# Two layers on one core: the counts of a search on TensorE, another layout of B, and the loads and stores at both ends

## The chip, the core and the metric

The kernel is one program on one core of a Trainium2 chip. Its metric is the time of one execution on the device, in microseconds (us). Engines are called as in the profile: PE (TensorE), PEld (its weight loads), DVE (VectorE), ACT (ScalarE), POOL (GpSimd), SP (SyncE, which here issues the DMAs that are not by index).

## The reference

The input is 8 sequences of 256 tokens with 128 channels, 2048 tokens in all, in float32. Two layers follow each other. Each normalizes its tokens (mean and variance over the channels), gives the result to an attention-like part and to a mixture of experts, and adds both to its input:

```
xn = layernorm(x)
x  = x + attn0(xn) + ffn0(xn)
xn = layernorm(x)
x  = x + attn1(xn) + ffn1(xn)
```

`attn0` is a state-space scan: a second layer norm, an up-projection to 256 channels, a causal convolution over 4 tokens and a silu give `xm`. From `xm` one product gives `delta` (softplus, 256 channels) and B and C (16 numbers each for every token). For each channel and each of 16 states a first-order recurrence runs over the 256 tokens of a sequence:

```
h = exp(delta*A) * h + xm * (exp(delta*A) - 1) / (delta*A) * delta * B
y = sum over the 16 states of C * h
```

`y` times a gate goes through a down-projection. `ffn0` has 8 experts, and each expert chooses its 512 best tokens by softmax score; its output, times the score, is added to those rows. `attn1` is a retention with 8 heads, a decay mask, a norm by head and a gate. `ffn1` has 16 experts, and each token goes to its two best.

## The kernel before

**Start (L184–L330).** The 2048 tokens lie as 16 columns of 128 partitions (`x`, tile of 128x16x128; token = column*128 + partition). Four DMAs load x (L187), then SP goes on with A_log and the weights (L124). DVE takes statistics of each column (L233, L234), with the two operations on A between columns 7 and 8 (L231, L232); normalized copies are transposed on PE. The router's scores `sc` (128x8x16, experts by columns) are ready at the end of this stage (L740 and the lines after it).

**The search (`search`, L428–L455).** The 512 best tokens of each of 8 experts are found by looking for the threshold score bit by bit, 3 bits a step, in ten steps. A step has 7 candidates for each expert. DVE forms them (`cand`, L431), compares all scores with all candidates (`ge`, 128 x 7x8x16, bf16, L435) and sums over the 16 columns (`cp`, L441). The generator yields here; when it is called again, PE sums over the partitions with one product with a matrix of ones (`pc`, L444), and DVE keeps the candidates with at least 512 tokens (`keep`, L449), counts them (`m`, L452) and sets three bits of the threshold (L453). `cand` and the threshold live in unused columns of the PSUM tile `py`, which PE's sums over the states also write. In the profile they appear as `py`.

**Fronts (`front(q)`).** The tokens are worked in four blocks q of 512 (two sequences each). A front computes what the scan needs of one block: `pu` (L314, up-projection and convolution in one), `pg` (L327, the gate), `pd` (L353, for delta), and `pbc` (B and C, copied to `BC`, 32x512, L368). `C` goes to DRAM (`C_d`, L369), whence SP loads it again spread over all partitions (`Cb`, L644). `BT` holds B by tokens: partition r of 128, 8 chunks of 64 tokens, 18 numbers each. Rows 0 to 63 hold the 64 tokens of a chunk with their 16 values at columns 2 to 17, rows 64 to 127 hold the same 64 tokens with their values at columns 0 to 15; a window of two columns then gives each half of the partitions its own two of four states. The front fills it with 16 products of 16x64 with the identity (`pbt`, L383, 8 chunks for each half of the partitions), and two copies on ACT (L388). After that come the transposes of `xm` (`pxT`, L393), the copy `xT` on ACT (L401) and two DMAs (L402, L403) that write `xS`, which is `xT` with its halves of the partitions swapped. On ACT the logarithm of softplus (`w`, L375) stands ahead of the copies of BT; on DVE its operand `z` (L374) stands ahead of it. POOL and DVE finish `delta` (L406, L408).

**Units of the scan.** A unit is one sequence b, four states g and 128 channels dc: 64 units, and 8 for each sequence. `spread_b` (POOL, L657) puts columns of BT on diagonals (`Bd`), PE multiplies them by xT and xS (`u`, L673), ACT computes the decays (`ab`, L684, four exponentials), DVE computes `u` (L692) and runs the recurrence (`h`, L696), POOL multiplies it by `Cb` (L700), and PE adds the states up (`py`, L709). `down` (L726) follows for each sequence.

**Order.** In this layer the order on PE, ACT, DVE and POOL is that of the program, written out by hand; each engine takes its instructions in that order, and SP its DMAs too. Front 0 runs before the loop, and at every second of its yields, up to the tenth, the search does a step. Then the loop runs over the units k. It issues unit k's `u` and `h`, the products of k+1, the sums of k−2, C of k−1, the decays and `Cb` of k+2 and `Bd` of k+4, and then one part of each generator that runs: the search until it is done, the front of the next block (from k = 0, 16 and 32), the selection of an expert's rows (`select`, one begun every 5 units), whose tokens POOL gathers (`xg`, L548), and the experts' products, whose results POOL adds to rows of `acc_d` (L572).

PSUM tiles named by `bank(...)` take turns in two buffers: pu, pg, pd, pbt, pxT and pc are among them.

**Second layer (L866 and on).** Retention, then 47 tiles of 128 rows through the 16 experts. The rows come back by index into `y_d` (L1221), two for each token. POOL also scatters the rows to their tiles (L1150).

**End (L1305–L1315).** `x1` is a tile of 128x16x128, laid out as `x` was. For each of four quarters SP loads the two outputs for its tokens (`y`, L1311, 256 KB each), after all scatters; DVE adds them (L1314); SP stores the quarter (L1315).

Of the kernel before, what the change touches and what calls it, by code (L numbers as in the profile page):

```python
# [10 lines left out]
BF16 = mybir.dt.bfloat16  # L11
AF = mybir.ActivationFunctionType
ALU = mybir.AluOpType
AX = mybir.AxisListType
PSUM = bass.MemoryType.PSUM

P = 128
NB = 8
L = 256
NT = NB * L  # L20
NC = NT // P
DM = 128
D = 256
ND = D // P
N = 16
K = 4
E0 = 8
# [16 lines left out]
BK = 64  # L44
# [6 lines left out]
def block_kernel(ctx: ExitStack, tc: tile.TileContext, a: dict, out: bass.AP):  # L51
    nc = tc.nc

    def bc(ap, axis, n):
# [16 lines left out]
    ident = const.tile([P, P], F32, name="ident")  # L71
# [6 lines left out]
        out=triu, in_=ones, compare_op=ALU.is_gt, fill=0.0, base=0,  # L78
# [7 lines left out]
    ones_b = const.tile([P, P], BF16, name="ones_b")  # L86
# [52 lines left out]
    def after_all(i, *groups):  # L139

        for g in groups:
            for j in g:
                tc.add_manual_dep(
                    i.ins, j.ins.name,
                    mybir.DependencyInfo(mybir.DependencyClass.Sync, mybir.DependencyReason.DATA),
                    reason="rows by index",
                )


    with ExitStack() as l0:  # L150
        ET = mybir.EngineType
        l0.enter_context(tc.manual_schedule(engines={ET.PE, ET.Activation, ET.DVE, ET.Pool}))
        main = l0.enter_context(tc.tile_pool(name="main", bufs=1))
# [8 lines left out]
        def bank(name, shape):  # L162
            return ps_m.tile(shape, F32, name=name, tag="m")
# [18 lines left out]
            return load(*args, pool=main)  # L182

        x = main.tile([P, NC, DM], F32, name="x", tag="c8")  # L184
        xv = a["x"].rearrange("(c p) d -> p c d", p=P)
        for q in range(4):
            nc.sync.dma_start(x[:, 4 * q : 4 * q + 4, :], xv[:, 4 * q : 4 * q + 4, :])  # L187
        alog = load0("alog", [P, ND, N], a["alog"].rearrange("(c p) n -> p c n", p=P))
# [10 lines left out]
        NK = (1 << SB) - 1  # L199
# [74 lines left out]
        for h in range(2):  # L274
            for g in range(2):
                q = 2 * h + g
# [26 lines left out]
        def front(q):  # L303
            cols = slice(q * BLK, (q + 1) * BLK)
            win = slice(2 * q, 2 * q + 2)
            xq = main.tile([P, ND, BLK], F32, name=f"xm{q}", tag="xm")
# [69 lines left out]
            BTq = main.tile([P, 8, N + 2], F32, name=f"BT{q}", tag="BT", bufs=2)  # L376
            BT[q] = BTq

            pbt = bank(f"pbt{q}", [P, 8, N + 2])
            own = [(slice(0, BK), slice(2, N + 2)), (slice(BK, P), slice(0, N))]  # L380
            for rows, at in own:
                for j in range(8):
                    nc.tensor.matmul(  # L383
                        pbt[rows, j, at], BC[0:N, j * BK : (j + 1) * BK], ident[0:N, 0:N],
                        start=True, stop=True,
                    )
            for rows, at in own:
                nc.scalar.copy(BTq[rows, :, at], pbt[rows, :, at])  # L388
            for i in range(2):
                px = bank(f"pxT{q}_{i}", [P, 2, D])  # L390
                for c in range(2):
# [37 lines left out]
        def search():  # L429
            for i in range(30 // SB):  # L430
                nc.vector.tensor_tensor(  # L431
                    cand, bc(thr, 1, NK), bc(bits[:, i, :], 2, E0), ALU.bitwise_or
                )
                ge = main.tile([P, NK, E0, NC], BF16, name=f"ge{i}", tag="ge")
                nc.vector.tensor_tensor(  # L435
                    ge, bc(sc, 1, NK), bc(cand.bitcast(F32), 3, NC), ALU.is_ge
                )

                cp = main.tile([P, NK, E0], BF16, name=f"cp{i}", tag="cp", bufs=2)
                with nc.allow_low_precision(reason="whole numbers up to 16"):  # L440
                    nc.vector.tensor_reduce(cp, ge, AX.X, ALU.add)  # L441
                yield
                pc = bank(f"pc{i}", [P, NK, E0])
                nc.tensor.matmul(  # L444
                    pc.rearrange("p k e -> p (k e)"), ones_b, cp.rearrange("p k e -> p (k e)"),
                    start=True, stop=True,
                )
                keep = main.tile([P, NK, E0], I32, name=f"keep{i}", tag="keep", bufs=2)
                nc.vector.tensor_scalar(keep, pc, CAP - 0.5, None, ALU.is_ge)  # L449
                m = main.tile([P, E0], I32, name=f"m{i}", tag="m", bufs=2)  # L450
                with nc.allow_low_precision(reason="whole numbers up to 7"):
                    nc.vector.tensor_reduce(m, keep.rearrange("p k e -> p e k"), AX.X, ALU.add)  # L452
                nc.vector.scalar_tensor_tensor(  # L453
                    thr, m, 30 - SB * (i + 1), thr, ALU.logical_shift_left, ALU.bitwise_or
                )  # L455
# [847 lines left out]


    yv = y_d[0 : 2 * NT, :].rearrange("(k p c) d -> p k c d", p=P, k=2)  # L1305
    ov = out.rearrange("(c p) d -> p c d", p=P)
    for q in range(4):
        y = work.tile([P, WB], F32, name=f"y{q}", tag="wb", bufs=AHEAD)
        y = y[:, 0 : 8 * DM].rearrange("p (k c d) -> p k c d", k=2, c=4)
        for k in range(2):  # L1310
            after_all(nc.sync.dma_start(y[:, k], yv[:, k, quarter[q], :]), put)  # L1311
        xq = x1[:, quarter[q], :]
        for k in range(2):
            nc.vector.tensor_add(xq, xq, y[:, k])  # L1314
        nc.sync.dma_start(ov[:, quarter[q], :], xq)  # L1315


# [70 lines left out]
def _layout(i):  # L1388
    import numpy as np

    c = lambda v: np.ascontiguousarray(np.asarray(v))
    t = lambda v: np.ascontiguousarray(np.asarray(v).T)
    wll, bll = np.asarray(i["L0_attn_W_ll"]), np.asarray(i["L0_attn_b_ll"])
    return {
        "x": c(i["L0_attn_X"]).reshape(NT, DM),
        "ln_g": c(i["L0_attn_ln_g"]).reshape(DM, 1),
        "ln_b": c(i["L0_attn_ln_b"]).reshape(DM, 1),
        "wup1": t(i["L0_attn_W_up1"]),
        "wup2": t(i["L0_attn_W_up2"]),
        "conv_w": t(c(i["L0_attn_conv_w"]).reshape(D, K)),  # L1400
        "bits": np.array(
            [[(k + 1) << (30 - SB * (j + 1)) for k in range((1 << SB) - 1)] for j in range(30 // SB)],
            np.int32,
        ),
        "conv_b": _columns(i["L0_attn_conv_b"]),
        "wll": t(wll),
        "bll_d": _columns(bll[:D]),
        "bll_bc": c(bll[D:]).reshape(2 * N, 1),
        "b2x": _blocks(i["L0_ffn_b2"]),
        "alog": c(i["L0_attn_A_log"]),  # L1410
        "wdown": t(i["L0_attn_W_down"]),
        "bdown": c(i["L0_attn_b_down"]),
        "wr0": c(i["L0_ffn_Wr"]),
        "w1_0": c(i["L0_ffn_W1"]),
        "b1_0": _columns(i["L0_ffn_b1"]),
        "w2_0": c(i["L0_ffn_W2"]),
        "wq0": _heads(i["L1_attn_Wq"], 0),
        "wq1": _heads(i["L1_attn_Wq"], 1),
        "wk0": _heads(i["L1_attn_Wk"], 0),
        "wk1": _heads(i["L1_attn_Wk"], 1),  # L1420
        "wvT": t(_heads(i["L1_attn_Wv"], None)),
        "cen": np.eye(P, dtype=np.float32) - _mean(),
        "avg": _mean(),
        "w1a": c(i["L1_attn_W1"]),
        "w2a": c(i["L1_attn_W2"]),
        "gn_w": c(i["L1_attn_gn_w"]).reshape(DM, 1),
        "gn_b": c(i["L1_attn_gn_b"]).reshape(DM, 1),
        "decay": _decay(),
        "wr1": c(i["L1_ffn_Wr"]),
        "br1": c(i["L1_ffn_br"]),  # L1430
        "bank": _banks(i["L1_ffn_W1"], i["L1_ffn_b1"], i["L1_ffn_W2"]),
        "b2_1": c(i["L1_ffn_b2"]),
    }
# [18 lines left out]
```

## Time and profile before

| what | value |
|---|---|
| time before, median of 6 runs | 687.72 us |
| lowest and highest of them | 683.97 and 691.09 us |
| time of the profiled execution | 686.88 us |
| span of the profiled execution | 685.2 us |
| mean granted clock of PE | 0.869 |
| cp (L441) | 10 of 1.09 us on DVE |
| pc (L444) | 10 products of 0.19 us |
| pbt (L383), block 0 | 32 PE rows, 3.19 us |
| copies of BT (L388) | 2 a block, 0.52 us together (block 3) |
| the last addition (L1314) begins | 681.20 us |

The profile is of one execution, taken by the hardware profiler. Its span is what the engines' records cover, and the time beside it is that execution's own; the median is over other executions. A row of a timeline gives start, duration, engine, line, operation, output and inputs, shapes and the count; brackets give the idle time of the engine before it and what ended that. Matmuls are pipelined, and a product in float32 shows as two matmuls. The granted clock is TensorE's, as a share of full speed. "q" behind an engine's name means its queue of DMA issues. The lines of the profile are shown in the prediction.

### The profile page before, as it was taken

The numbers are of one execution on the slowest core, as the hardware profiler recorded it, in microseconds if no ns is written. First come the engines' busy times: TensorE is split into PE (matmuls) and PEld (weight loads), VectorE is DVE, ScalarE is ACT, GpSimd is POOL, SyncE is SP. The second block draws the span as 40 slices with busy tenths as digits, with TensorE's granted clock in tenths as the row PEclk, the third lists the DMA queues.
The fourth block names the chain that finished last, engine by engine and source line by source line (L and its number), as shares of the span: only waits on it lengthen the run. The fifth ranks groups of instructions, "written<-read, shape, count | busy, mean of one in ns | idle before, by whom it ended". The sixth has DMA issues, their size and how long they took to land.

```text
span 685.2 us, 14527 instructions
## 1 busy us (share of the span) xinstructions
PE 546.0 (80%) x5721; PEld 415.7 (61%) x5721; DVE 432.0 (63%) x669; ACT 332.2 (48%) x763; POOL 383.8 (56%) x320
## 2 busy tenths in 40 slices
PE   0897768779989889979887975496449989999980
PEld 0666555667755667755766764353125579999880
DVE  7377898997855777756868695664026543554343
ACT  2646346447487756687763750262003234555430
POOL 5004555686988789977899895107730023344240
PEclk9996798889999899999999997577558899999995
DMA  7914001222396242332332220124215237888305
GB/s 210 109 24 124 32 32 55 91 93 82 84 199 138 82 101 71 94 93 69 91 97 50 72 68 6 62 93 157 95 59 155 94 112 261 269 302 299 112 28 188
DMA packets 59859, 76.27 MB, mean 111 GB/s; under 512 B 14992, under 2 KB 43808, under 8 KB 59536
## 3 DMA queue, kind: packets, MB, share of 16 engines
q1 hardware_dynamic: 51632, 65.81, 33.2%
q0 software_dynamic: 8160, 9.54, 6.5%
q8 instruction: 45, 0.74, 0.4%
q14 instruction: 22, 0.18, 0.1%
HBM read 59.46 MB, written 13.78 MB: 107 GB/s over the span
## 4 chain that ended last, share of the span: by engine, by line
PE 50%; DVE 20%; ACT 8%; issue 8%; another core or an unknown queue 6%; POOL 3%; DMA 3%; SPq 1%; DVEq 0%; POOLq 0%; ACTq 0%
PE ph L1201 6%; PE py L709 5%; PE py L1215 5%; PE u L673 5%; DVE h L696 5%; PE ph L606 4%; DVE u L692 4%; PE pu L314 4%; PE po L624 2%; ACT ab L684 2%; PE pd L353 2%; POOL h L700 2%; PE ps L1034 2%; DVE st L1041 2%
## 5 line engine op out<-in xcount | busy, mean ns | idle before, releaser
L700 POOL TENSOR_TENSOR h<-h,Cb 128x1024 f32<-128x1024 f32 x64 | 169.5, 2744 | 35.2 <-DVE h L696 19.9
L696 DVE TENSOR_TENSOR_SCAN h<-ab,u 128x1024 f32<-128x1024 f32 x64 | 146.3, 2287 | 5.9
L684 ACT ACTIVATE ab<-delta,An 128x256 f32<-128x256 f32 x256 | 108.5, 497 | 19.3 <-DVE h L696 18.5
L1221 POOL DMA_INDIRECT y_d<-yo,xt x47 | 45.5, 968 | 118.6 <-DVE yo L1220 105.4
L692 DVE SCALAR_TENSOR_TENSOR u<-ab,u 128x1024 f32<-128x1024 f32 x64 | 77.8, 1216 | 37.9 <-ACT ab L684 14.8
L709 PE MATMUL py<-h,dg 64*64 64x128 f32 x2048 | 78.9, 295 | 18.3 <-POOL h L700 12.5
L673 PE MATMUL u<-Bd,xT 64*128 64x128 f32 x512 | 81.1, 304 | 14.4 <-DVE h L696 14.0
L673 PEld LDWEIGHTS u<-Bd,xT 64*128 64x128 f32 x512 | 68.6, 206 | 25.2 <-issue 9.7
L709 PEld LDWEIGHTS py<-h,dg 64*64 64x64 f32 x2048 | 62.4, 145 | 33.1 <-POOL h L700 17.0
L673 PE MATMUL u<-Bd,xS 64*128 64x128 f32 x512 | 79.3, 305 | 1.8 <-DMA xS<-xT 1.8
L1206 ACT ACTIVATE hid<-ph,wb 128x128 f32<-128x128 f32 x188 | 53.5, 368 | 48.7 <-issue 20.4
L673 PEld LDWEIGHTS u<-Bd,xS 64*128 64x128 f32 x512 | 66.6, 206 | 2.1 <-DMA xS<-xT 2.1
L1041 DVE TENSOR_TENSOR st<-ps,decay_sb 128x384 f32<-128x384 f32 x64 | 31.1, 547 | 55.6 <-remote 32.3
L572 POOL DMA_INDIRECT acc_d<-oc,idx x32 | 51.5, 1609 | 16.9 <-ACT oc L629 8.6
L1150 POOL DMA_INDIRECT xs_d<-xk,pos x32 | 32.0, 1001 | 41.9 <-DVE hit L1132 32.5
L1201 PE MATMUL ph<-xT,wb 128*128 128x128 f32 x376 | 52.9, 286 | 2.9 <-DVE xT L1195 2.7
L657 POOL TENSOR_TENSOR Bd<-eye,BT 128x256 f32<-128x256 f32 x64 | 52.4, 1051 | 0.0
L1201 PEld LDWEIGHTS ph<-xT,wb 128*128 128x128 f32 x376 | 48.0, 200 | 5.9 <-DVE xT L1195 3.1
L1215 PE MATMUL py<-wb,hid 128*128 128x128 f32 x376 | 49.5, 275 | 0.0
L624 PE MATMUL po<-w,ht 128*128 128x128 f32 x256 | 39.5, 296 | 10.8 <-ACT z L358 2.6
L624 PEld LDWEIGHTS po<-w,ht 128*128 128x128 f32 x256 | 33.8, 199 | 22.1 <-ACT ht L611 8.1
L1215 PEld LDWEIGHTS py<-wb,hid 128*128 128x128 f32 x376 | 45.7, 192 | 0.0
(257 smaller groups left out, 896.8 us busy)
## 6 DMA issues: line engine op xcount, KB each, us to landing
wb<-in_bank_dram SPq DMA_DIRECT2D x47, 514.0 KB
Cb<-C_d SPq DMA_DIRECT2D x32, 512.0 KB
w<-in_w_dram SPq DMA_DIRECT2D x16, 256.0 KB
xs_d<-zrow SPq DMA_DIRECT2D x1, 3031.5 KB
xt<-xs_d SPq DMA_DIRECT2D x11, 260.0 KB
xS<-xT SPq DMA_DIRECT2D x16, 128.0 KB
y<-y_d SPq DMA_DIRECT2D x8, 256.0 KB
decay_sb<-in_decay_dram SPq DMA_DIRECT2D x1, 1536.0 KB
```

Of the source, the lines that this page charges most:

```text
L572: i = nc.gpsimd.indirect_dma_start(out=acc_d, out_offset=bass.IndirectOffsetOnAxis(ap=idx[:, e, s : s + 1], axis=0), in_=oc, in_offset=Non ...
L624: nc.tensor.matmul(po, ht[:, hc, s * P : (s + 1) * P], w2[:, hc, :], start=(hc == 0), stop=(hc == NH - 1),)
L657: nc.gpsimd.tensor_tensor(t[:, w], eye.unsqueeze(1).unsqueeze(1).to_broadcast([P, 2, 2, BK]), bc(BT[b // 2][:, j + 2 * i : j + 2 * i + 2, ...
L673: nc.tensor.matmul(U[k][:, 2 * r : 2 * r + 2, t0 : t0 + BK], xT[b][r ^ half][rows, c, dc * P : (dc + 1) * P], Bd[b, g][rows, 2 * c + half] ...
L684: nc.scalar.activation(ab[k][:, n, :], delta[b // 2][:, dc, (b % 2) * L : (b % 2 + 1) * L], AF.Exp, scale=An[:, dc, g * NG + n : g * NG + ...
L692: nc.vector.scalar_tensor_tensor(U[k], ab[k], -1.0, U[k], ALU.add, ALU.mult)
L696: return nc.vector.tensor_tensor_scan(hf, af, uf, 0.0, ALU.mult, ALU.add)
L700: nc.gpsimd.tensor_mul(hh[k][:, w], hh[k][:, w], Cb[b, g][:, w])
L709: nc.tensor.matmul(pyv[cols, i, dc, :], dg[rows, dc, g * NG + n, :], hh[k][rows, n, j * P : (j + 1) * P], start=(g == 0 and dc == 0 and n ...
L1201: nc.tensor.matmul(ph[:, hc, :], w[:, hc * P : (hc + 1) * P], xTs[t], start=True, stop=True)
L1206: nc.scalar.activation(hids[t][:, hc, :], ph[:, hc, :], AF.Relu, bias=w[:, DI + NH * DM + hc : DI + NH * DM + hc + 1],)
L1215: nc.tensor.matmul(py, hids[t][:, hc, :], w[:, DI + hc * DM : DI + (hc + 1) * DM], start=(hc == 0), stop=(hc == NH - 1),)
```

## The change

1. The search no longer sums over the columns on DVE (`cp` and L441 go). PE forms `pc` with 16 products that add up in PSUM, one for each column of `ge`; the moving operand of each has 56 numbers in steps of 16 (32 bytes apart). They stand where the one product stood.
2. `pbt` is made by four products of 128 tokens, all partitions at once, in place of 16 of 64. A chunk with an even number then lies in rows 0 to 63, one with an odd number in rows 64 to 127. ACT copies each to its own half of BT, and two DMAs on SP (64 partitions, 4 pieces of 64 bytes each) copy each half's chunks to the other half.
3. At the end, the eight loads of y are issued ahead of the four stores, and the four quarters of y are held at once.
4. The input and the output are handed over by partition: a partition's share of x (16 tokens of 128) is contiguous in DRAM, and so is a partition's share of the output. The reordering lies outside of the kernel's time.

```diff
--- before.py
+++ after.py
@@ -182,7 +182,7 @@
             return load(*args, pool=main)
 
         x = main.tile([P, NC, DM], F32, name="x", tag="c8")
-        xv = a["x"].rearrange("(c p) d -> p c d", p=P)
+        xv = a["x"]
         for q in range(4):
             nc.sync.dma_start(x[:, 4 * q : 4 * q + 4, :], xv[:, 4 * q : 4 * q + 4, :])
         alog = load0("alog", [P, ND, N], a["alog"].rearrange("(c p) n -> p c n", p=P))
@@ -376,16 +376,17 @@
             BTq = main.tile([P, 8, N + 2], F32, name=f"BT{q}", tag="BT", bufs=2)
             BT[q] = BTq
 
-            pbt = bank(f"pbt{q}", [P, 8, N + 2])
-            own = [(slice(0, BK), slice(2, N + 2)), (slice(BK, P), slice(0, N))]
-            for rows, at in own:
-                for j in range(8):
-                    nc.tensor.matmul(
-                        pbt[rows, j, at], BC[0:N, j * BK : (j + 1) * BK], ident[0:N, 0:N],
-                        start=True, stop=True,
-                    )
-            for rows, at in own:
-                nc.scalar.copy(BTq[rows, :, at], pbt[rows, :, at])
+            pbt = bank(f"pbt{q}", [P, 4, N])
+            for c in range(4):
+                nc.tensor.matmul(
+                    pbt[:, c, :], BC[0:N, c * P : (c + 1) * P], ident[0:N, 0:N],
+                    start=True, stop=True,
+                )
+            up, low = slice(0, BK), slice(BK, P)
+            nc.scalar.copy(BTq[up, 0:8:2, 2:], pbt[up])
+            nc.scalar.copy(BTq[low, 1:8:2, 0:N], pbt[low])
+            nc.sync.dma_start(BTq[up, 1:8:2, 2:], BTq[low, 1:8:2, 0:N])
+            nc.sync.dma_start(BTq[low, 0:8:2, 0:N], BTq[up, 0:8:2, 2:])
             for i in range(2):
                 px = bank(f"pxT{q}_{i}", [P, 2, D])
                 for c in range(2):
@@ -435,16 +436,14 @@
                 nc.vector.tensor_tensor(
                     ge, bc(sc, 1, NK), bc(cand.bitcast(F32), 3, NC), ALU.is_ge
                 )
-
-                cp = main.tile([P, NK, E0], BF16, name=f"cp{i}", tag="cp", bufs=2)
-                with nc.allow_low_precision(reason="whole numbers up to 16"):
-                    nc.vector.tensor_reduce(cp, ge, AX.X, ALU.add)
                 yield
                 pc = bank(f"pc{i}", [P, NK, E0])
-                nc.tensor.matmul(
-                    pc.rearrange("p k e -> p (k e)"), ones_b, cp.rearrange("p k e -> p (k e)"),
-                    start=True, stop=True,
-                )
+                for c in range(NC):
+                    nc.tensor.matmul(
+                        pc.rearrange("p k e -> p (k e)"), ones_b,
+                        ge.rearrange("p k e c -> p (k e) c")[:, :, c],
+                        start=(c == 0), stop=(c == NC - 1),
+                    )
                 keep = main.tile([P, NK, E0], I32, name=f"keep{i}", tag="keep", bufs=2)
                 nc.vector.tensor_scalar(keep, pc, CAP - 0.5, None, ALU.is_ge)
                 m = main.tile([P, E0], I32, name=f"m{i}", tag="m", bufs=2)
@@ -1303,15 +1302,18 @@
 
 
     yv = y_d[0 : 2 * NT, :].rearrange("(k p c) d -> p k c d", p=P, k=2)
-    ov = out.rearrange("(c p) d -> p c d", p=P)
+    ov = out.rearrange("(p c) d -> p c d", p=P)
+    ys = []
     for q in range(4):
         y = work.tile([P, WB], F32, name=f"y{q}", tag="wb", bufs=AHEAD)
         y = y[:, 0 : 8 * DM].rearrange("p (k c d) -> p k c d", k=2, c=4)
         for k in range(2):
             after_all(nc.sync.dma_start(y[:, k], yv[:, k, quarter[q], :]), put)
+        ys.append(y)
+    for q in range(4):
         xq = x1[:, quarter[q], :]
         for k in range(2):
-            nc.vector.tensor_add(xq, xq, y[:, k])
+            nc.vector.tensor_add(xq, xq, ys[q][:, k])
         nc.sync.dma_start(ov[:, quarter[q], :], xq)
 
 
@@ -1392,7 +1394,7 @@
     t = lambda v: np.ascontiguousarray(np.asarray(v).T)
     wll, bll = np.asarray(i["L0_attn_W_ll"]), np.asarray(i["L0_attn_b_ll"])
     return {
-        "x": c(i["L0_attn_X"]).reshape(NT, DM),
+        "x": c(c(i["L0_attn_X"]).reshape(NC, P, DM).transpose(1, 0, 2)),
         "ln_g": c(i["L0_attn_ln_g"]).reshape(DM, 1),
         "ln_b": c(i["L0_attn_ln_b"]).reshape(DM, 1),
         "wup1": t(i["L0_attn_W_up1"]),
@@ -1448,4 +1450,5 @@
     with tile.TileContext(nc) as tc:
         block_kernel(tc, args, out)
     r = _run(nc, [arrays], core_ids=[0])
-    return r.results[0]["out_0_dram"].reshape(NB, L, DM)
+    y = r.results[0]["out_0_dram"].reshape(P, NC, DM)
+    return y.transpose(1, 0, 2).reshape(NB, L, DM)
```

## The prediction

> **What bounds the kernel now.** Three views, in this order: the page's busy shares and chain of waits; the timeline of the scan loop's first units, where the search runs; the timelines around B's copies and at the end.
>
> ```profile
> PE 546.0 (80%) x5721; PEld 415.7 (61%) x5721; DVE 432.0 (63%) x669; ACT 332.2 (48%) x763; POOL 383.8 (56%) x320
> PE 50%; DVE 20%; ACT 8%; issue 8%; another core or an unknown queue 6%; POOL 3%; DMA 3%; SPq 1%; DVEq 0%; POOLq 0%; ACTq 0%
> ```
>
> TensorE carries half of the chain, VectorE a fifth. Work moved from VectorE to TensorE gains only where VectorE ends last. All three parts touch short stretches, so I read each stretch by itself. The search runs at 35–101 us; this is one unit of the scan loop with one step in it:
>
> ```profile
> 85.08 1.09 DVE L435 TENSOR_TENSOR ge<-sc,py 128x896 bf16<-128x896 f32 x1
> 86.20 1.09 DVE L441 TENSOR_REDUCE cp<-ge 128x56 bf16<-128x896 bf16 x1
> 86.31 1.10 PE L709 MATMUL py<-h,dg 64*64 64x128 f32 x32 [1.19 <-POOL h L700]
> 87.20 1.22 DVE L692 SCALAR_TENSOR_TENSOR u<-ab,u 128x1024 f32<-128x1024 f32 x1
> 87.35 1.99 PE L314 MATMUL pu<-XnT,wcv 128*128 128x256 f32 x8
> 88.59 2.29 DVE L696 TENSOR_TENSOR_SCAN h<-ab,u 128x1024 f32<-128x1024 f32 x1
> 89.18 0.19 PE L444 MATMUL pc<-cp,ones_b 128*128 128x56 bf16 x1
> 90.80 0.19 DVE L449 TENSOR_SCALAR keep<-pc 128x56 int32<-128x56 f32 x1
> ```
>
> (Columns: start, duration, engine, line, output and inputs, count, and in brackets the idle time before and what ended it.) The count waits on PE behind py and pu, and ends at 89.37, 1.43 us before the scan lets DVE reach keep. So DVE sets this unit, with 1.09 us of cp in its row.
>
> **The change part by part.**
>
> *Count products.* Each of ten steps loses cp (1.09 us on DVE) and its one product becomes 16 accumulating ones: 15 more weight loads and matmuls a step, 150 of each in all, at the same place in PE's order. A bf16 product read in steps of 32 bytes is nowhere in this trace. The nearest row is
>
> ```profile
> 131.59 0.57 PE L535 MATMUL pi<-rr,ol 128*32 128x32 bf16 x16
> ```
>
> 16 bf16 products with 32 weight and 32 moving columns, spaced (0.57−0.176)/15 = 0.026 us. With 128+56 columns in place of 32+32 that is 0.026×184/64 = 0.076 us, my value: 15×0.076 = 1.13 us a step at full clock, 2.27 at half. The low end is the row itself (0.026, 0.4 us a step); the high end is the router's L740, whose fp32 products cost 6.83/32 = 0.213 us (3.2 us a step). I take the scaled row, since its type and form are nearest.
>
> [...]
>
> Before the loop (front of block 0, 35.7–63.6 us) PE is the path: pu, pc, pu, pc, pg, pd follow without gaps but for keep (0.32 and 0.34 us), as pg and pd wait for the PSUM bank that keep releases. The first count has 0.96 us of slack before the next pu (+0.2); the next two shift everything by 1.1 each: +2.2 up to BC at 55.03. From there DVE gains cp back: z no longer stands behind cp at 56.68, so the logarithm behind it on ACT comes 2.2−1.09 = 1.1 later, and so do the copies of BT. Taken on below.
>
> In the loop five steps remain (counts at 70.08, 73.58, 83.84, 89.18, 97.55). DVE's row a unit with a step goes from 6.9 to 5.8. PE's row is not free to run ahead: py writes the PSUM tile that holds the candidates, so it waits for ge. From keep: 2.1 us to the end of ge, py 1.05 (2.0 at half clock), pu 2.0 (2.85), pc 0.2: 5.35, or 7.15 at half clock. With 15 more products: 6.5 or 9.4. So before the larger is 6.9 (7.15), after 6.5 (9.4): −0.45 at full clock, +2.2 at half; one unit without pu in it −1.1; the first unit, still on PE's path at half clock, +1.0. The granted clock was 0.50 at 57–68, 0.85 at 74–77, 0.50 at 77–80, 0.63 at 80–84, 1.00 at 84–93, 0.66 at 93–98 us. Over the five I get **+0.2** (−4.4 with 0.026 us everywhere, +5 at 0.12). It breaks even where 15 spacings eat the 6.9−5.35 = 1.55 us: 0.10 us a product.
>
> *B.* 16 products of 64x16 become four of 128x16, 32 PE rows become 8; ACT's two copies halve; two DMAs of 64 partitions with 4 pieces of 64 bytes swap the halves. They go on SP's queue before the four xS transfers and behind Cb where Cb is due, and Bd on POOL waits for them.
>
> Block 0: pbt 3.19 us, on PE's path, becomes about 1.06 (L393's four products at the same clock). But ACT copies BT only after the logarithm, so the xT copy comes at 60.6 instead of 60.02, SP has two more issues of some 0.55 us ahead of xS, and the landing (2.32 us) follows: +1.2, and +0.3 for the 512 small pieces ahead in the DMA queues: **+1.5** for front 0 with its counts (+0.4 to +5). Block 1: pbt is 2.79 us of the chain, at half clock; Bd needs BT only at 145, so the DMA is hidden: **−0.6** (0 to −1.4).
>
> Blocks 2 and 3 have no such cover. Block 3:
>
> ```profile
> 330.48 0.52 ACT L388 COPY BT<-pbt 64x128 f32<-64x128 f32 x2
> 332.28 2.95 POOL L700 TENSOR_TENSOR h<-h,Cb 128x1024 f32<-128x1024 f32 x1
> 334.59 2.75 POOL L657 TENSOR_TENSOR Bd<-eye,BT 128x256 f32<-128x256 f32 x2
> 335.25 0.32 SPq L644 DMA_DIRECT2D Cb<-C_d  x1
> 335.62 0.47 SPq L402 DMA_DIRECT2D xS<-xT  x1
> 338.56 2.96 POOL L700 TENSOR_TENSOR h<-h,Cb 128x1024 f32<-128x1024 f32 x1
> ```
>
> Cb's issue waits until POOL's h (to 335.23) frees its buffer; the BT transfers now queue behind it on SP, start at 335.6 and 336.1, and land some 2.3 us later (xS's time) at 338.4. POOL's Bd waits for that, about 3 us after 335.2; queued behind it on POOL are a scatter at 337.50 and h at 338.56, whose py on PE (343.12) has 1.6 us of slack. POOL is busy 45.91 of 49 us there, and in 340–375 PE waits for its h six times, 7.9 us in all. So the stall mostly arrives: **+2** (0 to +3). Block 2 is the same at 237.1–240.1, but the h at 243.02 has 4.5 us of slack before its py (250.49): **+1** (0 to +3), for the two gathers and the scatter also queued. pbt's saving there is not on the path.
>
> *Input layout.* x arrives in rows of 2 KB instead of 512 bytes. At 3–6 us the old rows moved at 267–311 GB/s, at 673–674 the 2 KB rows of y at 381. The normalization's DVE row starts at 3.81 on x and waits 0.36 for An behind A_log, queued behind x: **−0.55** (0 to −0.8).
>
> *Tail.*
>
> ```profile
> 674.88 0.39 SPq L1315 DMA_DIRECT2D out_dram<-x  x1
> 675.36 0.46 SPq L1311 DMA_DIRECT2D y<-y_d  x1
> 676.66 0.39 SPq L1315 DMA_DIRECT2D out_dram<-x  x1
> 677.10 0.52 SPq L1311 DMA_DIRECT2D y<-y_d  x1
> 678.20 4.10 SPq L1315 DMA_DIRECT2D out_dram<-x  x2
> 681.20 0.69 DVE L1314 TENSOR_TENSOR x<-x,y 128x512 f32<-128x512 f32 x1 [0.95 <-DMA y<-y_d]
> ```
>
> The seventh and eighth loads stand on SP behind stores that wait for additions, and their data share the DMA engines (busy 0.85–1.01) with those stores. Loading all first, 2.1 MB at 300–340 GB/s from 671.3 end at 677.5–678.3; the last addition ends about 0.7 later, at 678.2–679.6 instead of 681.89. The 3.3 us from there to the span's end stay: **−2.7** (−1.5 to −3.5).
>
> *Sum:* +1.5 +0.2 −0.6 +1.0 +2.0 −0.55 −2.7 = **+0.85 us**. Against the profiled execution's own 686.88 that is 687.7, which is also the median of the runs before (687.72, they spread from 683.97 to 691.09).
>
> **The rivals.**
>
> *Faster, the products are cheap.* Spacing is near the 0.026 row, PE's extra work keeps the clock up, DVE sets four units at −1.1, POOL's stalls vanish in slack: front 0 +0.4, units −4.4, block 1 −0.6, blocks 2 and 3 +1, ends −3.3: −6.9, **680**. For it: that row. Against: 128 weight columns are loaded anew for each product.
>
> *Slower, the row of counts becomes the bound.* From 0.10 us a product on, PE is late in every unit with a step; at 0.12: three units at full clock +0.25, one at half +3.65, front 0 +3, and the two POOL stalls in full +6, block 1 and the ends −3.9: +9.5, **696.4**. For it: the half clock in 57–68, 77–80 and part of 93–98; POOL's fullness at 326–375. Against: it was 1.00 at 84–93.
>
> *The waiting stretch moves.* At 475–503 us DVE (32.3 us) and ACT wait on POOL's 32 scatters. The change does not touch it, yet a shifted start could move it by 10 us either way; no row argues a direction.
>
> *Only the two ends move.* The search and B hide behind other work or cancel exactly, and the layouts and the tail remain: −0.55−2.7 = −3.25, **683.6**. For it: POOL and PE have slack in most units after 101 us. Against: the stall of block 3 has 1.6 us of cover for 3.
>
> **How the numbers follow.** Forecast (sum near zero, 684.3–691.1): 0.37. Cheap products: 0.23. Only the ends: 0.07. Row of counts, with both POOL stalls in full: 0.29. The moved stretch: 0.04, half each way. A measurement of this kernel tells about 0.5% (3.4 us) from no change. So faster is 0.23+0.07+0.02 = 0.32, within 0.37, slower 0.29+0.02 = 0.31. The range of 8 in 10 runs from just inside the cheap case to just short of the slow one, 681 to 695.5: each end cuts off about 0.1.
>
> **What would show it.** The spacing of the 16 products at pc: 0.03, 0.08 or over 0.1 us decides the first part. Right if keep in the loop's units waits for pc at half clock and not at 84–93; if POOL's first Bd of blocks 2 and 3 waits for a DMA; if the first u waits for xS about 1.5 us later; if the eight y loads stand together on SP and the last addition ends near 679. I am wrong if the clock pattern of 57–98 us changes altogether, or if a stretch after 101 us that no part touches differs by over 3 us.

## The result and the profile after

The changed kernel takes 697.97 us (median of 20 runs), the kernel before 688.05 us (46 runs beside them): a ratio of 1.0163, 95% interval 1.0139 to 1.0187, so 1.4 to 1.9% slower. The forecast was 687.7 us with a range up to 695.5. It was wrong. The profiled execution has a span of 698.8 us, 13.6 more than the one before (single executions scatter; for sizes the ratios count). Some executions take longer, mostly at a lower granted clock of PE (one of the changed kernel 704.59 us at 0.865, its others at 0.868 to 0.889); the ratios leave them out, and the traces of b_act_queue and b_blocks01, whose profiled executions were of that kind, are not used below.

The page of the changed kernel, busy shares and chain:

```profile
PE 555.5 (79%) x5775; PEld 425.6 (61%) x5775; DVE 421.5 (60%) x659; ACT 331.9 (48%) x763; POOL 381.2 (55%) x320
PE 49%; DVE 20%; ACT 9%; issue 8%; another core or an unknown queue 5%; POOL 4%; DMA 3%; SPq 0%; DVEq 0%; POOLq 0%; ACTq 0%
```

DVE lost 10.5 us of work (cp, ten times 1.09) and PE gained 9.5, yet the span grew by more than either. The shares don't show where. One row of each unit does: the recurrence h on DVE. Its 64 starts in the two traces, after less before:

| unit of the scan | h starts later by, us |
|---|---|
| 0 (first) | 7.12 |
| 2 | 6.26 |
| 3 | 8.79 |
| 5 (the search is over) | 11.03 |
| 5 to 16 | 11.02 to 11.03 |
| 28 / 34 (before and after block 2's B) | 10.30 / 10.84 |
| 44 / 50 (before and after block 3's B) | 9.52 / 14.71 |
| 63 (last) | 13.42 |
| end of the span | 13.6 |

So 11 us come before unit 5, where the search runs, and then nothing for 50 us, in which the trace of the changed kernel repeats that of before to 0.01 us. A row that exists once for each unit, lined up in both traces, tells where time is lost before any cause is guessed.

For blocks 2 and 3 the table shows too little, because the profiled execution of before had a standstill of its own there. In its chain:

```profile
238.19 5.50 another core or an unknown queue
```

In loads_first (below), whose code is the same at this place, the matching wait is 1.76 us, and the scans of before fall 3.6 us behind those of loads_first between units 28 and 29. Held against loads_first, the changed kernel loses 6.9 us from unit 28 to unit 63.

The 7.12 us of the first scan are not all the change's either. The first pu, ahead of every count, took longer in the changed kernel (before first, then after):

```profile
35.54 5.18 PE L314 MATMUL pu<-XnT,wcv 128*128 128x256 f32 x16
```
```profile
35.79 6.66 PE L314 MATMUL pu<-XnT,wcv 128*128 128x256 f32 x16
```

In the sixteen traces used this row takes 5.13 to 6.66 us, whatever the kernel. From there the changed kernel's chain runs over the counts to the transfers of BT; its end (start, duration, piece):

```profile
56.97 1.83 PE pbc L364 x4
58.81 1.76 PE pc L442 x16
60.59 0.23 DVE keep L448
61.60 1.09 DVE ge L436
62.68 1.15 DVE z L374
63.86 1.06 ACT w L375
65.96 3.60 DMA BT<-BT
```

The timelines of DVE and of PE in one unit with a search step, to be held against the unit shown for before:

```profile
85.39 1.09 DVE L436 TENSOR_TENSOR ge<-sc,py 128x896 bf16<-128x896 f32 x1
86.39 1.22 DVE L691 SCALAR_TENSOR_TENSOR u<-ab,u 128x1024 f32<-128x1024 f32 x1
87.78 2.29 DVE L695 TENSOR_TENSOR_SCAN h<-ab,u 128x1024 f32<-128x1024 f32 x1
93.99 0.22 DVE L448 TENSOR_SCALAR keep<-pc 128x56 int32<-128x56 f32 x1 [3.92 <-PE pc L442]
```
```profile
86.62 1.98 PE L708 MATMUL py<-h,dg 64*64 64x128 f32 x32 [0.91 <-DVE ge L436]
88.53 3.78 PE L314 MATMUL pu<-XnT,wcv 128*128 128x256 f32 x8
92.11 1.84 PE L442 MATMUL pc<-ge,ones_b 128*128 128x56 bf16 x16
```

cp is gone and u follows ge at once, as meant. But keep, which before came as soon as the scan ended, now waits 3.92 us for pc. PE's row has become the bound: py cannot start before ge, py and pu run here at half clock (1.98 and 3.78 us at a granted clock of 0.50, before 1.10 and 1.99 at 1.00), and pc takes 1.84 us instead of 0.19.

The granted clock can be read beside pc. Two steps, their rows and the windows inside them (columns: stretch, length, busy time and count of PE, PEld, DVE, ACT, POOL, granted clock, share of the DMA engines, GB/s):

```profile
76.96 1.82 PE L442 MATMUL pc<-ge,ones_b 128*128 128x56 bf16 x16
```
```profile
66.30:67.70 1.40, 1.40 (x16) 1.40 (x15) 1.21 (x1) 0.74 (x2) 0.00 (x0) 0.50 0.27 34
76.96:78.40 1.44, 1.44 (x16) 1.44 (x15) 0.00 (x0) 1.24 (x4) 1.44 (x1) 1.00 0.00 0
```

The step at 66.2 us ran at a clock of 0.50 and took 1.84 us; the one at 77 us ran at 1.00 and took 1.82. All ten lie between 1.81 and 1.84. The time of these products did not follow PE's granted clock; what holds them at (1.82−0.28)/15 = 0.10 us each (0.28 is the median of one), no run shows.

In B, POOL's first Bd waits for the DMAs in three of the four blocks, 13.8 us in all. The row of Bd before and after:

```profile
L657 POOL TENSOR_TENSOR Bd<-eye,BT 128x256 f32<-128x256 f32 x64 | 52.4, 1051 | 0.0
```
```profile
L656 POOL TENSOR_TENSOR Bd<-eye,BT 128x256 f32<-128x256 f32 x64 | 48.9, 958 | 13.8 <-DMA BT<-BT 13.8
```

And the end, SP and DVE:

```profile
683.60 4.01 SPq L1311 DMA_DIRECT2D y<-y_d  x8
688.49 7.40 SPq L1317 DMA_DIRECT2D out_dram<-x  x4
692.12 3.42 DVE L1316 TENSOR_TENSOR x<-x,y 128x512 f32<-128x512 f32 x5 [3.05 <-DMA y<-y_d]
```

The eight loads stand together now, but the last addition ends 11.94 us after the first load's issue, against 11.91 before.

### The profile page after: what moved, and what is told of

Its sections match the earlier page's. It is cut to its first block, busy times and chain, and to the rows that moved or that the text cites. A ratio compares the mean times of both kernels' runs of the same rounds, so it can differ in the third digit from the quotient of the medians.

```text
span 698.8 us, 14645 instructions
## 1 busy us (share of the span) xinstructions
PE 555.5 (79%) x5775; PEld 425.6 (61%) x5775; DVE 421.5 (60%) x659; ACT 331.9 (48%) x763; POOL 381.2 (55%) x320
## 4 chain that ended last, share of the span: by engine, by line
PE 49%; DVE 20%; ACT 9%; issue 8%; another core or an unknown queue 5%; POOL 4%; DMA 3%; SPq 0%; DVEq 0%; POOLq 0%; ACTq 0%
PE py L708 6%; PE ph L1200 5%; PE py L1214 5%; PE pu L314 4%; PE ph L605 4%; PE u L672 4%; DVE h L695 4%; DVE u L691 4%; ACT ab L683 3%; PE po L623 3%; PE ps L1033 2%; PE pc L442 2%; POOL h L699 2%; DVE st L1040 2%
## 5 line engine op out<-in xcount | busy, mean ns | idle before, releaser
L683 ACT ACTIVATE ab<-delta,An 128x256 f32<-128x256 f32 x256 | 108.4, 497 | 16.2 <-DVE h L695 13.8
L656 POOL TENSOR_TENSOR Bd<-eye,BT 128x256 f32<-128x256 f32 x64 | 48.9, 958 | 13.8 <-DMA BT<-BT 13.8
L1200 PE MATMUL ph<-xT,wb 128*128 128x128 f32 x376 | 51.5, 281 | 3.3 <-DVE xT L1194 2.7
L1200 PEld LDWEIGHTS ph<-xT,wb 128*128 128x128 f32 x376 | 46.6, 195 | 5.8 <-DVE xT L1194 3.1
L623 PE MATMUL po<-w,ht 128*128 128x128 f32 x256 | 38.1, 291 | 9.6 <-ACT BT L387 3.9
```

Of the source, the lines that this page charges most:

```text
L623: nc.tensor.matmul(po, ht[:, hc, s * P : (s + 1) * P], w2[:, hc, :], start=(hc == 0), stop=(hc == NH - 1),)
L656: nc.gpsimd.tensor_tensor(t[:, w], eye.unsqueeze(1).unsqueeze(1).to_broadcast([P, 2, 2, BK]), bc(BT[b // 2][:, j + 2 * i : j + 2 * i + 2, ...
L683: nc.scalar.activation(ab[k][:, n, :], delta[b // 2][:, dc, (b % 2) * L : (b % 2 + 1) * L], AF.Exp, scale=An[:, dc, g * NG + n : g * NG + ...
L1200: nc.tensor.matmul(ph[:, hc, :], w[:, hc * P : (hc + 1) * P], xTs[t], start=True, stop=True)
```

## The experiments

The first theory after the result (S) was that the strided products are the main cost; its rivals were a fixed price of each product, whatever it reads, and the DMA wait for B (theory B). The kernels do parts of the change alone, starting from the kernel before, or mend one of them. They ran in five groups, each on one chip beside the kernel before, which took 685.6 and 683.3 us in two groups and 648.6 to 649.2 in three (why is not known); so ratios are compared, never total times across groups.

| kernel | what differs from before | ratio | 95% interval |
|---|---|---|---|
| (the change) | all | 1.0163 | 1.0139–1.0187 |
| search_only | 16 products a step | 1.0097 | 1.0062–1.0133 |
| b_only | B | 1.0058 | 1.0021–1.0094 |
| ends_only | layouts and end | 0.9968 | 0.9933–1.0003 |
| search_contig | 16 products, ge written for them | 1.0266 | 1.0211–1.0322 |
| search_cmajor | 16 products, ge worked columns outermost | 0.9941 | 0.9909–0.9973 |
| loads_first | loads ahead of stores only | 0.9972 | 0.9947–0.9996 |
| b_act_queue | B, DMAs issued by ACT | 1.0051 | 1.0017–1.0085 |
| after_cmajor | all, ge as in search_cmajor | 1.0030 | 1.0000–1.0060 |
| cmajor_ends | search_cmajor and the ends | 0.9962 | 0.9924–1.0000 |
| b_blocks01 | B in blocks 0 and 1 | 0.9999 | 0.9966–1.0032 |
| b_blocks23 | B in blocks 2 and 3 | 1.0093 | 1.0059–1.0127 |
| b_cb_late | B, Cb issued later | 1.0101 | 1.0054–1.0149 |
| cb_late | Cb issued later | 0.9995 | 0.9969–1.0021 |
| cmajor_loads | search_cmajor and loads first | 0.9918 | 0.9887–0.9949 |
| b_act_23 | b_blocks23, DMAs issued by ACT | 1.0016 | 0.9985–1.0047 |
| cmajor_b_act_ends | all, both repairs | 0.9999 | 0.9973–1.0026 |

**The parts by themselves.** search_only, b_only and ends_only are the hunks of the diff, each alone.

> Before, with only the count products of the change (no cp, 16 products a step). Theory S: the strided count products are the main cost. In the changed kernel's trace a step's 16 products took 1.82 us at a granted clock of 1.00 and 1.84 at 0.50, against 0.19 for one, so 1.62 us a step; the first scan of the loop comes about 5 us later than before (four counts ahead of it on PE's path, less about 1.1 for cp) and the units up to 5 lose about 4 more: +8 us, near 696. Theory B (the DMA wait for B is the main cost): this kernel loses at most 4 us, near 692 or less. If the search also moves PE's clock pattern, the units at 80 to 100 us show a granted clock of 0.5 where before had 1.00.

> Before, with only the B part (4 products, two DMAs that swap halves). Theory S: +1 to +3 us, since the DMAs land 3.6 us after their start (the changed kernel's first one) and hold POOL's Bd in block 0 by some 1.7 us and in block 3 by about 3, less 0.6 in block 1: 688 + 2 = 690. Theory B: +5 or more, 693 and up, with block 3 alone at +3 to +4. The trace is read for the idle time of POOL at the first Bd of each block, ended by a DMA of BT.

> Before, with only the layouts of x and of the output and the eight y loads ahead of the stores. The forecast said -3.25 us (684.8 beside 688.05). The changed kernel's profile speaks for no gain: from the first y load to the last addition's end it has 11.94 us, before 11.91, and the first statistics start 0.73 us later. So 0 within 0.7 by that; if the run shows -2 or less, the loads stalled in that one execution only.

The product of the three ratios is 1.0097·1.0058·0.9968 = 1.0123; with their intervals that meets the 1.0163 of the whole. The search costs 6.6 us and is the largest part, a little less than the 8 expected; B costs 4.0, between the two theories' numbers; the ends gain about 2 by the runs (from 4.6 gained to 0.2 lost), where one profile had shown nothing. Both halves of "search against B" have a share, so each was taken apart.

**What a count product costs.** search_contig keeps PE's order and changes only how ge lies:

```diff
-ge = main.tile([P, NK, E0, NC], BF16, ...)
+ge = main.tile([P, NC, NK, E0], BF16, ...)
-    ge, bc(sc, 1, NK), bc(cand.bitcast(F32), 3, NC), ALU.is_ge
+    ge.rearrange("p c k e -> p k e c"), bc(sc, 1, NK),
+    bc(cand.bitcast(F32), 3, NC), ALU.is_ge
-        ge.rearrange("p k e c -> p (k e) c")[:, :, c],
+        ge[:, c].rearrange("p k e -> p (k e)"),
```

> As search_only, but ge is laid out with the 16 columns outermost, so the 56 numbers that a product moves lie side by side (DVE writes them in the other order). Theory S (the step of 32 bytes is what costs): the spacing falls from 0.108 us to between 0.026 (the spacing of pi) and 0.077 us, a step costs 0.4 to 1.2 us, and the total is between 3 us faster and 3 us slower than before. Rival (each product has a fixed price, with its 128 weight columns loaded anew): the spacing stays near 0.108 and the total near that of search_only, +8. DVE's ge may take longer than 1.09 us in this order; if so that is read apart.

DVE and PE of one step in that kernel:

```profile
44.48 4.25 DVE L435 TENSOR_TENSOR ge<-sc,py 128x896 bf16<-128x896 f32 x1
```
```profile
48.79 0.59 PE L442 MATMUL pc<-ge,ones_b 128*128 128x56 bf16 x16 [1.81 <-DVE ge L435]
```

The same 16 products with the same 16 weight loads take 0.59 us, (0.59−0.19)/15 = 0.027 us each, the spacing of pi (0.026). The fixed price is refuted; the step of 32 bytes cost a factor of 0.10/0.027, nearly four. At half clock the step took longer, as its row and the window inside it (columns as above) show:

```profile
70.07 0.95 PE L442 MATMUL pc<-ge,ones_b 128*128 128x56 bf16 x16
```
```profile
70.10:71.00 0.90, 0.90 (x18) 0.82 (x16) 0.90 (x1) 0.59 (x1) 0.90 (x2) 0.50 0.07 18
```

The window holds 18 matmuls in 0.90 us at a granted clock of 0.50; in that from 42.90 to 43.40 us of the same trace, at 1.00, there are 17 in 0.50 us. So with a contiguous read the time of these products did move with PE's clock. But the total went to +18 us, outside both expectations: DVE now writes with a step of 112 bytes, and ge takes 4.25 us instead of 1.09. The price had moved to the other engine.

search_cmajor lets DVE work in the order in which it writes, from the scores before they are turned:

```diff
-    ge, bc(sc, 1, NK), bc(cand.bitcast(F32), 3, NC), ALU.is_ge
+    ge, bc(ex, 2, NK), bc(cand.bitcast(F32), 1, NC), ALU.is_ge
```

> As search_only, but ge has the columns outermost and DVE also works in that order, from the scores as they lie before they are turned (ex, column by expert), so both the write of ge and the 56 numbers that a product moves are contiguous. Theory S (the step costs, on PE where PE reads with it, on DVE where DVE writes with it): ge stays at 1.09 us, the 16 products take about 0.6 at full clock as in search_contig, and the gain that was meant appears: cp's 1.09 us leaves DVE's row in some four units and the first front loses at most 0.5 a step: 2 to 5 us faster than before. Rival (ge is slow in any order with the columns outermost): ge near 4.25, the total near search_contig, +20.

A unit of it, DVE and then PE:

```profile
82.63 0.22 DVE L447 TENSOR_SCALAR keep<-pc 128x56 int32<-128x56 f32 x1 [1.43 <-PE pc L441]
83.64 1.09 DVE L435 TENSOR_TENSOR ge<-ex,py 128x896 bf16<-128x896 f32 x1
86.03 2.29 DVE L694 TENSOR_TENSOR_SCAN h<-ab,u 128x1024 f32<-128x1024 f32 x1
```
```profile
82.02 0.57 PE L441 MATMUL pc<-ge,ones_b 128*128 128x56 bf16 x16
```

ge is back at 1.09 us, pc at 0.57, keep waits 1.43 us instead of 3.92 (a part of that is pu, which takes 2.52 us in this unit and 3.78 in the other, there at a granted clock of 0.50), and the kernel is 0.6% faster than before. The idea of the search's part was sound; one layout decides whether it gains 0.6% or loses 1%. after_cmajor puts that layout into the whole change:

> The changed kernel whole, but with ge laid out and worked columns outermost as in search_cmajor. Theory S with the parts adding up: ratio 0.9941 (search_cmajor) times 1.0058 (b_only) times 0.9968 (ends_only) = 0.9967, so about 2 us faster than before, within 0.4%; against the changed kernel as given (1.0163) it gains 1.9%. Rival (the parts work on each other, and something else in the whole costs): above 1.004.

It takes 1.3% off the whole (1.0163 to 1.0030), not the 1.9 expected; its interval lies between the two expectations and reaches both. A part of what is left is B in block 0: the first scan starts at 69.49 us, in search_cmajor at 67.67, behind a Bd that waited 3.63 us for BT (1.82 in b_only). Bd started 3.9 us after the second transfer did, in b_only 2.1; why the transfers took longer is open.

**Where B costs.** In b_only, POOL and SP at block 3, to be held against the lines of before:

```profile
333.10 2.96 POOL L701 TENSOR_TENSOR h<-h,Cb 128x1024 f32<-128x1024 f32 x1
339.93 1.19 POOL L658 TENSOR_TENSOR Bd<-eye,BT 128x256 f32<-128x256 f32 x2 [3.87 <-DMA BT<-BT]
342.33 2.93 POOL L701 TENSOR_TENSOR h<-h,Cb 128x1024 f32<-128x1024 f32 x1
```
```profile
336.08 0.32 SPq L645 DMA_DIRECT2D Cb<-C_d  x1
336.45 0.62 SPq L388 DMA_DIRECT2D BT<-BT  x1
337.12 0.62 SPq L389 DMA_DIRECT2D BT<-BT  x1
```

The sequence is the forecast's: Cb is issued when POOL's h ends, the two transfers follow, POOL stands still for 3.87 us, and the next h starts 9.2 us after the last, before 6.3. Splitting B by blocks (an `if q < 2` around old and new code) places it:

> Before, with the B part in blocks 0 and 1 only. If B's cost is the stall of block 3 (POOL's Bd of block 3 waited 3.87 us for the DMA in b_only, and the scans stood 3.1 us later behind it), this kernel is at 1.000 to 1.002; if it is the first front, where POOL waited 1.82 us, it keeps most of b_only's 1.0058. The scans of b_only stood +0.83 at the first unit and -0.55 at units 3 to 16.

> Before, with the B part in blocks 2 and 3 only. By the stall of block 3: 1.004 to 1.006, with the last scan 3 to 4 us later against the first. By the first front: 1.000 to 1.002.

Blocks 0 and 1 cost nothing measurable, blocks 2 and 3 cost 0.6 to 1.3%. To tell SP's order from the transfers, b_act_queue issues them elsewhere:

```diff
-nc.sync.dma_start(BTq[up, 1:8:2, 2:], BTq[low, 1:8:2, 0:N])
-nc.sync.dma_start(BTq[low, 0:8:2, 0:N], BTq[up, 0:8:2, 2:])
+nc.scalar.dma_start(BTq[up, 1:8:2, 2:], BTq[low, 1:8:2, 0:N])
+nc.scalar.dma_start(BTq[low, 0:8:2, 0:N], BTq[up, 0:8:2, 2:])
```

> As b_only, but ACT issues the two DMAs right behind its two copies, so they do not stand behind Cb on SP. Theory Q (the place on SP's queue, behind a Cb that waits for POOL, makes block 3's stall): the DMAs start at 331.6 instead of 336.45, land about 2.8 later, before POOL's h ends at 336; POOL's Bd of block 3 waits for no DMA, and the total is 0 to +1.5 over before, against +4 for b_only. Rival (the landing itself is what costs, wherever it starts): still +3 to +5. ACT's issues may cost some 0.6 us each on ACT.

The total stayed at 1.0051, about 3 us, which speaks for the rival. The two theories were then tried on SP itself, with the next Cb's issue moved behind the fronts' step, and with that move alone as a control:

> b_only, but in each turn of the loop Cb is issued behind the fronts' step, so on SP the transfers of BT and xS no longer stand behind a Cb that waits for POOL's h. Theory Q (SP's order makes the cost of B in blocks 2 and 3): POOL's first Bd of block 3 waits for no DMA of BT, the scans of units 44 to 56 keep their distance (in b_only they lost 3.3 us, in b_blocks23 2.3), and the total is that of cb_late, within 0.3%. Rival (the two transfers cost by themselves): 0.4% or more over cb_late.

> Before, with only the issue of Cb moved behind the fronts' step: the control for b_cb_late. xS of blocks 1 to 3 starts earlier, Cb a little later; both had slack, so 0 within 0.3%.

b_cb_late failed as a test. The Cb that stands before the transfers had been issued a turn earlier, so the order on SP was the old one (Cb at 332.93, BT at 333.30 and 333.97), and Bd waited 3.90 us again. It is a repeat of b_only beside a good control: from unit 28 to unit 63 its scans fall 6.3 us behind those of cb_late, in two steps, at blocks 2 and 3. The test that answers is b_act_23:

> b_blocks23, but ACT issues the two DMAs behind its copies, so no Cb stands before them. Theory Q (the place on SP's queue behind Cb): the scans keep their distance over blocks 2 and 3 (b_act_queue lost 0.95 us over the whole layer against loads_first on the same chip, b_cb_late 5.2 against cb_late), and the ratio is 0.998 to 1.003, against 1.0093 for b_blocks23. Rival (the transfers cost by themselves wherever they start): 1.005 or more.

Its ACT and POOL at block 3:

```profile
326.18 0.60 ACTq L389 DMA_DIRECT2D BT<-BT  x1
326.82 0.63 ACTq L390 DMA_DIRECT2D BT<-BT  x1
```
```profile
326.92 2.95 POOL L713 TENSOR_TENSOR h<-h,Cb 128x1024 f32<-128x1024 f32 x1
329.70 1.31 POOL L670 TENSOR_TENSOR Bd<-eye,BT 128x256 f32<-128x256 f32 x2
333.02 2.94 POOL L713 TENSOR_TENSOR h<-h,Cb 128x1024 f32<-128x1024 f32 x1
```

Bd follows h with no wait for a DMA, h comes 6.1 us after h, and the ratio is 1.0016 (0.9985–1.0047), apart from the 1.0093 (1.0059–1.0127) of b_blocks23. From unit 28 to unit 63 its scans keep their distance to those of loads_first (within 0.4 us at the end), while those of b_blocks23 fall 5.0 us behind. The two ratios come from groups of different speed, but b_cb_late, whose group was as quick as that of b_act_23, still cost 1.0101. In blocks 2 and 3 the cost is the place on SP's queue. Why B in all four blocks with ACT's queue stays at 1.0051 is not settled: block 0 is the candidate, since in cmajor_b_act_ends, where ACT issues the transfers, Bd of block 0 still waits 4.34 us for BT and the first scan starts at 70.60 us; but b_blocks01, at 0.9999 with SP's queue, does not show it.

**The end, and versions to keep.**

> Before, with only the order at the end changed: eight y loads, then the four stores, both layouts as before. If the forecast's mechanism holds without the layouts, -2.7 (the last addition ends 9.2 us after the first load's issue, before 11.9). If the end is set by the 3.15 MB that loads and stores move together at some 280 GB/s, whatever their order, 0 within 0.5, with the last addition again 11.5 to 12.2 us after the first issue.

> search_cmajor with the two ends, and B left as before: the version that the runs so far point to. The product of the two ratios is 0.9941 * 0.9968 = 0.991, 6 us faster than before; if the ends add nothing beside it, 0.994.

> search_cmajor with the loads ahead of the stores and the layouts as before: the product of the two ratios measured, 0.9941 * 0.9972 = 0.991, within 0.4%. If the new layouts carry a part of the gain at the end, it is behind cmajor_ends (0.9962).

> The changed kernel with both repairs: ge worked columns outermost, and the DMAs for B issued by ACT. Theory Q: after_cmajor (1.003) less most of B's cost, 0.996 to 0.999; if ACT's issue does not help, 1.003 again. cmajor_ends, without the B part, stood at 0.9962.

From the first y load's issue to the span's end the seven traces with the loads first have 14.0 to 15.2 us (mean 14.7), the nine with the old order 15.1 to 16.4 (mean 15.6): 0.9 us gained, and loads_first has the gain without any layout. It falls short of the forecast: the last addition ends 10.8 us after the first load's issue, between the 9.2 of the forecast and the 11.5 of its rival. The layouts show no gain: the two traces without them have the two shortest ends (14.0 and 14.2 us, the five others 14.6 to 15.2), and cmajor_ends, with them, missed its 0.991. cmajor_loads, with neither B nor the layouts, met its 0.991 and has the lowest ratio: 0.8% faster than before (0.5 to 1.1%), 2.4% faster than the change by the ratios' quotient; the intervals of search_cmajor and cmajor_ends overlap with its own. cmajor_b_act_ends lies between its two expectations and decides for neither.

## Why the prediction was wrong, step by step

- **The spacing of the count products: the step that failed.** The prediction scaled pi's row by columns to 0.076 us and then by the clock (1.13 us a step at full, 2.27 at half). Measured: 0.10 us and 1.63 us more a step at either clock; and pi's own 0.026 us holds once the read is contiguous, so the columns were the wrong scale, and for a read in steps the clock was too. The row it was scaled from differed in the one property that mattered: how the moving operand lies. The same 16 products take 0.10 us each in steps of 32 bytes (the change) and 0.027 contiguous (search_contig), a factor of nearly four. The prediction said that no row of its trace reads in such steps, and its value held no price for them.
- **Front 0 (+1.5).** Measured +6.9 in the profiles (7.12 less 0.24 that the start brought), of which 1.5 is the longer first pu, which no part of the change touches. The search is the largest piece of the rest: search_only, with a pu as short as before, has its first scan 3.82 us later. The three counts ahead of BC moved PE by 0.8, 1.2 and 1.6 us, not by 0.2, 1.1 and 1.1. A fourth count, behind pbc, was left out; it is on the path through keep, ge and z to the copies of BT, so cp's 1.09 us did not come back there. And the transfers of BT landed 3.60 us after the second's start, not 2.3. The first u waited not for xS, as forecast, but for Bd and so for BT.
- **The five units (+0.2).** Measured +3.9 (7.12 to 11.03), inside the bounds given (−4.4 to +5). The break-even of 0.10 us a product was worked out right, for full clock: in search_only the unit from keep at 89.61 to keep at 96.56 us, at a granted clock of 1.00, takes 6.95 us, against 6.9 before. The rest goes with the places where the clock falls to half, and these moved: in 84–88 and 88–93 us it was 1.00 and 1.00 before, 0.77 and 0.50 in the change, 0.69 and 1.00 in search_only, whose five units lose only 1.2 us with the same products. That keep would wait for pc at half clock was a sign named beforehand, and it waited 3.92 us; a clock pattern that changes was named as a sign of being wrong. (The prediction's prices by unit add up to +1.2 with one unit wholly at half clock; how it came to +0.2 it does not say.)
- **Block 1 (−0.6).** Nothing: the scans keep 11.02 to 11.03 through it. pbt was on the listed chain, but its saving went into slack.
- **Blocks 2 and 3 (+1 and +2).** The mechanism was right to the row: Cb, then BT, landing some 3 us late, POOL's Bd waiting, h behind it. The size was somewhat low: b_only's whole cost is 4.0 us (1.4 to 6.4), b_blocks23's 6.4 (4.0 to 8.7), against +3 for these two blocks.
- **Start (−0.55).** The first statistics began at 4.54 instead of 3.81 us, and rows of 2 KB brought the first quarter of x later, not earlier: the five traces with this layout begin at 4.43 to 4.54 us, the eleven others at 3.52 to 4.01. PE's first router product came 0.24 later (29.10 us), which is within the scatter of the kernels without the layout (28.62 to 29.43).
- **End (−2.7).** About −0.9 by the traces. The prediction took 300 to 340 GB/s for the loads once the stores stood behind; in the changed kernel's profile the rate fell to 107 GB/s at 688–690 us, with all loads issued. Why it falls is open.
- **The rival that came true.** "Row of counts": decides from 0.10 us a product, 696.4 us. The measured 0.10 sits at its threshold and the time 1.6 us above its price. It had 0.29, less than a forecast whose central number came from scaling an unlike row; the range ended at 695.5, just short of the rival's own price. That its sum came so near is in part luck: front 0 was +6.9 for its +3, and the ends about −0.9 for its −3.3.

## What to carry to other kernels

When work moves to an engine that is to read it in steps, price the step before the operation: the same 16 products cost 0.59 or 1.82 us, and writing for them in steps cost DVE 4.25 instead of 1.09; in search_cmajor's order, contiguous for both, the two cost 0.57 and 1.09. Two small transfers behind Cb on SP's queue left POOL's Bd of block 3 waiting for 3.87 us (b_only), on ACT's queue for none (b_act_23): when a transfer is put on a queue, look at which engine frees the buffer of the DMA ahead, and who waits behind. And where a sum's largest term has no like row in the trace, the range should reach the price of the case beyond its break-even.

## What the runs showed of the hardware

- Products whose moving operand is bf16 in steps of 32 bytes took 1.82 us for 16 at a granted clock of 1.00 and 1.84 at 0.50 (the change); contiguous, 0.59 us in one step and 0.95 in one at 0.50 (search_contig). The strided read did not follow PE's clock in these rows.
- A compare on DVE with 896 results in bf16 took 1.09 us with contiguous writes (before, the change, search_cmajor) and 4.25 with a step of 112 bytes (search_contig).
- Behind two transfers inside the on-chip memory, each of 64 partitions with 4 pieces of 64 bytes, the reader started 2.8 us (block 3 of b_only), 3.8 and 4.9 us (blocks 0 and 3 of the change) after the second's start, with other transfers in flight.
